# Three series of node rows in every odd step of the sorting loop instead of two in each

## The chip, the cores and the metric

The kernel runs on one NeuronCore of a Trainium2 chip. The metric is the device time of one execution in microseconds. Before the change the median of three runs was 2923.28 us (2914.42 to 2926.03). One further execution was recorded by the hardware profiler, and all rows below come from that one.

## What is computed

There are 16 graphs of 1024 nodes with 64 channels and a 0/1 adjacency matrix each. Two layers follow one another:

```python
h = relu(layernorm(x))
# layer 0, for each node: drop every skip-th neighbour, then per channel
#   sort h over the remaining neighbours (and itself), take the quantiles 0.25, 0.5, 0.75,
#   weigh them 0.25, 0.5, 0.25  -> agg
x = x + (relu((h + agg) @ W1 + b1) @ W2 + b2) * mask
# layer 1: three graph convolutions x_i = bn(relu(adj @ (x_{i-1} @ W_i) + b_i)),
h = relu(layernorm(x))
x = x + relu(concat(x1, x2, x3) @ Wl + bl)
```

The costly part is the sort of layer 0: every node sorts the values of its own neighbours, channel by channel.

## The kernel before, in words

**Pairs, blocks and series.** Graphs are handled in eight pairs (p = 0 to 7). In each graph the nodes are ranked by their number of neighbours, and places of similar rank share one sorting network (`NETS`). Places 0 to 639 and 960 to 1007 are sorted as *blocks* (`BLOCKS`, with 11, 13, 15 and 26 slots), and 1008 to 1023 as the *tail* (42 slots): TensorE picks the neighbours' values with matmuls (`gather_words`, L1215, and `gather`, L1286; VectorE makes the picking matrices at L1190 and L1255), ScalarE copies them out, and VectorE sorts with `min` and `max` (`quantiles`, L1131; products and sums at L1143 and L1152). The places 640 to 959 are sorted as *series of node rows* (`NODES`): type 0 has 17 slots, type 1 has 19, type 2 has 21. Here GpSimd fetches the neighbours' rows with indirect DMAs (`fetch_nodes`, L1413), two *asks* for one slot, and a memset of `rest_row` (L1422) as a measured pause; one slot is complete after two asks and one memset. The list of rows to ask for (`rows_listed`, L769) is the last product of `prepare` for that pair. There are 20 series: type 0 and type 1 for each pair, type 2 for each two pairs. `NODE_ORDER` (L45) says in which order they are taken.

**The loop.** For p = 0 to 6 the loop does, one after the other on VectorE: block 0, a series, block 1, block 2, a second series, in p = 4 the tails of pairs 0 to 4 as well, and block MID (the fourth block). `weave` spreads other work between the instructions of a sort: the steps of `prepare` for the next pair (by `SHARES`), the gathers of later blocks, and the asks for the next series. `asking(fetched, first, end, share)` puts that share of a series' slots evenly between two points of the sort. The first ask of a slot also waits for the sorting instruction before it (`sorted_by`), so asks don't run ahead of the sort. Both series of a step use one buffer, with the tag `gn` in `rows`: the second can't be asked for before the first is sorted. The buffer `g1` holds block 1, and afterwards block MID.

In the loop of before (L1843 to L1861) the second series is asked for during block 1 (0.4 of it) and block 2 (the rest), the MID and tail gathers are woven into block 2, and the first series of the next step is asked for at the end (0.4 beside block MID, the rest beside the next block 0). Fourteen series are sorted in the loop.

**Behind the loop.** The last pair is sorted there, and with it six series, in buffers of their own (`r0`, and two of the tag `s`). Beside them `later` (L1604) runs what is left of both layers for all eight pairs, by `LATE_SHARES` steps for each sort and the remaining steps after the last one (`ahead.rest()`). The `later` work of a pair reads `agg_d`, into which the results are written by an indirect DMA of GpSimd (`scatter`, L1312). A result of a block goes through `store` (L1319): TensorE turns it, ScalarE copies it to one of three tiles `o` (L1332), and GpSimd scatters it from there.

**Order.** Each engine carries out its instructions in the order written into its queue; a waiting instruction holds all behind it. GpSimd's queue holds the asks, their memsets, the scatters into `agg_d`, and the scatters into `live_d` and loads of `lp` (L934, L949) that `prepare` needs.

Of the kernel before, what the change touches and what calls it, by code (L numbers as in the profile page):

```python
# [10 lines left out]
F32 = mybir.dt.float32  # L11
# [13 lines left out]
P = 128  # L25
C = 64
# [3 lines left out]
MIN_DEG = 10.0  # L30
TAUS = ((0.25, 0.25), (0.5, 0.5), (0.75, 0.25))

SHARES = (20, 22, 14, 30, 9)
LATE_SHARES = (8, 8, 8, 8, 9, 9, 10, 8, 11, 8, 8)

MAGIC = 8388608.0

# [5 lines left out]
NODES = ((640, 768, 14, 17), (768, 896, 16, 19), (896, 960, 17, 21))  # L43

NODE_ORDER = (  # L45
    ((0,), 0), ((0,), 1), ((1,), 0), ((1,), 1), ((0, 1), 2), ((2,), 0), ((2,), 1), ((3,), 0), ((3,), 1), ((2, 3), 2),
    ((4,), 0), ((4,), 1), ((5,), 0), ((5,), 1), ((4, 5), 2), ((6,), 0), ((6,), 1), ((6, 7), 2), ((7,), 0), ((7,), 1),
)

LISTED = 24  # L50
# [359 lines left out]
def graph_layers_kernel(ctx: ExitStack, tc: tile.TileContext, ins, out: bass.AP):  # L410
# [889 lines left out]
    def send(pools, after=None):  # L1300

        send_nodes()
        for one in waiting:
            store(*one, pools, after)
        waiting.clear()
# [94 lines left out]
    def fetch_nodes(pairs, i, pools, tag):  # L1400

        work, ps, rows = pools
        j0, j1, _, slots = NODES[i]
        G = len(pairs) if i == 2 else 2
        pool = work if tag == "s" else keep if tag == "r0" else rows
        g = pool.tile([P, slots, G * C], F32, tag=tag, bufs=2 if tag == "s" else 1, name="g_nodes")

        def ask():
            for k in range(slots):
                for a in range(G):  # L1410
                    st = pairs[a if i == 2 else 0]
                    at = 4 if i == 2 else 2 * a + i
                    asked = nc.gpsimd.indirect_dma_start(  # L1413
                        out=g[:, k, a * C : (a + 1) * C],
                        out_offset=None,
                        in_=rows_d[st.p][:, :],
                        in_offset=bass.IndirectOffsetOnAxis(ap=st.listed[:, at, k : k + 1], axis=0),
                    )
                    if rested[0] is not None:
                        follow(asked, rested[0])  # L1420
                    if a == G - 1:
                        rested[0] = nc.gpsimd.memset(rest_row, 0.0)  # L1422
                        follow(rested[0], asked)
                    if a == 0 and sorted_by[0] is not None:
                        tc.add_manual_dep(
                            asked.ins, sorted_by[0].ins.name,
                            mybir.DependencyInfo(mybir.DependencyClass.Sync, mybir.DependencyReason.DATA),
                            reason="rows are asked for one by one",
                        )
                yield  # L1430

        z = work.tile([P, len(TAUS), G], F32, tag="z_nodes", bufs=2, name="z_nodes")
        for a in range(G):
            st = pairs[a if i == 2 else 0]
            at = 4 if i == 2 else 2 * a + i
            nc.scalar.copy(z[:, :, a : a + 1], st.nodes_z[:, :, at : at + 1])
        return pairs, i, g, z, Steps(ask())
# [12 lines left out]
    def asking(fetched, first, end, share=1.0):  # L1450

        return fetched[4], math.ceil(share * NODES[fetched[1]][3]), first, end
# [357 lines left out]
    with ExitStack() as stack:  # L1810
        keep = stack.enter_context(tc.tile_pool(name="keep", bufs=1))
        pools = (
            stack.enter_context(tc.tile_pool(name="work", bufs=1)),
            stack.enter_context(tc.tile_pool(name="ps", bufs=1, space=PSUM)),
            stack.enter_context(tc.tile_pool(name="rows", bufs=1)),
        )
        with ExitStack() as inner:
            early = (
                inner.enter_context(tc.tile_pool(name="early", bufs=1)), keep,
                inner.enter_context(tc.tile_pool(name="ps_early", bufs=1, space=PSUM)),  # L1820
            )
            ahead = Steps(prepare(0, early))
            ahead.rest()
            load_weights()
            sts = [ahead.result]
            jobs = iter(NODE_ORDER)

            def fetch_next(tag="gn"):
                pairs, i = next(jobs)
                return fetch_nodes([sts[p] for p in pairs], i, pools, tag)  # L1830

            nodes = fetch_next()
            nodes[4].rest()
            first, *_ = gather_block(sts[0], 0, pools)
            first.rest()
            for p in range(NP - 1):
                st = sts[p]
                ahead = Steps(prepare(p + 1, early))

                def steps(n):  # L1840
                    return ahead, SHARES[n], 0.0, 1.0

                weave(sort_block(st, 0, pools), gather_block(st, 1, pools), asking(nodes, 0.0, 0.9), steps(0))  # L1843
                weave(sort_nodes(nodes, pools), gather_block(st, 2, pools), steps(1))
                nodes = fetch_next()
                weave(sort_block(st, 1, pools), asking(nodes, 0.1, 1.0, 0.4), steps(2))
                send_nodes()
                both = rows_of_pairs(MID, p, p + 1, p, pools, "g1")
                weave(
                    sort_block(st, 2, pools), gather_block(st, MID, pools, into=both),  # L1850
                    gather_block(st, MID + 1, pools, (early[0], "a", 2)), asking(nodes, 0.0, 0.7), steps(3),
                )
                if p in TAILS:
                    tails = rows_of_pairs(MID + 1, *TAILS[p], TAILS[p][1], pools, "g0")
                weave(sort_nodes(nodes, pools), steps(4))
                ahead.rest()
                sts.append(ahead.result)
                nodes = fetch_next()
                if p in TAILS:
                    weave(sort_pairs(MID + 1, *TAILS[p], tails, pools))  # L1860
                    send(pools)  # L1861
                weave(
                    sort_pairs(MID, p, p + 1, both, pools), gather_block(sts[-1], 0, pools, first=0.3, end=1.0),
                    asking(nodes, 0.0, 1.0, 0.4),
                )


        with ExitStack() as inner:
            one = inner.enter_context(tc.tile_pool(name="late", bufs=1))
            late = (one, inner.enter_context(tc.tile_pool(name="ps_late", bufs=2, space=PSUM)))  # L1870
            done = Pair()
            done.sent = 4
            ahead = Steps(later(late, keep, done))
            def steps(n):
                return ahead, LATE_SHARES[n], 0.0, 1.0

            st = sts[-1]
            weave(sort_block(st, 0, pools), gather_block(st, 1, pools), asking(nodes, 0.0, 0.9), steps(0))
            weave(sort_nodes(nodes, pools), gather_block(st, 2, pools), steps(1))
            nodes = fetch_next()  # L1880
            then = [fetch_next("r0")]
            weave(sort_block(st, 1, pools), asking(nodes, 0.0, 0.9), steps(2))
            send_nodes()
            both = rows_of_pairs(MID, NP - 1, NP, NP - 1, pools, "g1")
            weave(
                sort_block(st, 2, pools), gather_block(st, MID, pools, into=both), asking(then[0], 0.0, 0.9), steps(3)
            )
            tails = rows_of_pairs(MID + 1, *TAILS[NP - 1], NP - 1, pools, "g0")
            weave(sort_nodes(nodes, pools), gather_block(st, MID + 1, pools, into=tails[:, :, -TW:]), steps(4))
            then += [fetch_next(), fetch_next("s"), fetch_next("s")]  # L1890
            weave(
                sort_pairs(MID + 1, *TAILS[NP - 1], tails, pools), asking(then[1], 0.0, 0.5), asking(then[2], 0.5, 1.0),
                steps(5),
            )
            send(pools)
            done.sent = NP - 2
            weave(sort_nodes(then[0], pools), asking(then[3], 0.0, 1.0), steps(6))
            send_nodes()
            weave(sort_pairs(MID, NP - 1, NP, both, pools), steps(7))
            send(pools)  # L1900
            weave(sort_nodes(then[1], pools), steps(8))
            send_nodes()
            done.sent = NP - 1
            weave(sort_nodes(then[2], pools), steps(9))
            send_nodes()
            weave(sort_nodes(then[3], pools), steps(10))
            send(pools)
            done.sent = NP
            ahead.rest()
# [49 lines left out]
```

## Time and profile before

| what | value |
|---|---|
| median of three runs | 2923.28 us |
| the profiled execution | 2848.07 us, its span 2846.3 us |
| mean granted TensorE clock | 0.867 |
| VectorE (DVE) busy | 2302.2 us, 81% |
| TensorE (PE) busy | 2121.2 us, 75% |
| GpSimd (POOL) busy | 1740.8 us, 61% |
| ScalarE (ACT) busy | 1659.0 us, 58% |

How to read it: times within the profiled execution are microseconds from the start of its span. The loop's first sort begins at about 238, and its steps begin at 238, 491, 761, 1029, 1280, 1605 and 1863; the part behind the loop begins at 2116. A row of groups gives line, engine, operation, names and shapes, the count, busy time and the mean of one in ns, and then the time that the engine stood idle just ahead of it with what ended the idling. A row of waits gives who waited for what: total, number of times, and the longest.

### The profile page before, as it was taken

Reading aid. Unit: us, or ns where it says so; the run is one execution under the profiler, and the core shown is the slowest. Engines: PE = TensorE matmul, PEld = TensorE weight load, DVE = VectorE, ACT = ScalarE, POOL = GpSimd, SP = SyncE. Lnnn points to the kernel's source line nnn. Section 1 sums busy time; section 2 is a strip of 40 time slices with the busy share of each in tenths; the row PEclk is TensorE's granted clock in tenths of the full one; section 3 lists DMA queues with packets and bytes.
Section 4 is the critical chain, followed back from the end, with each engine's and each line's share of the span. In section 5 each row is a group of like instructions: output and inputs, shape, how many; then the busy total and the mean of one; then the engine's idle time right before and its main releaser. Section 6 shows DMA issues by size and latency. Waiting matters only on the chain. (4 is left out here: it accounts for less than half of the span.)

```text
span 2846.3 us, 54834 instructions
## 1 busy us (share of the span) xinstructions
PE 2121.2 (75%) x21210; PEld 1375.9 (48%) x21226; DVE 2302.2 (81%) x5388; ACT 1659.0 (58%) x3325; POOL 1740.8 (61%) x1568
## 2 busy tenths in 40 slices
PE   3658977796688589869852797599777999219888
PEld 2435554454455356546531555365545566115555
DVE  3138998898989989989979898999987899419963
ACT  4795877587657857785864487767751324003322
POOL 7126665486828765673867748748691788885100
PEclk9779987898889789889966898699879899659999
DMA  4214222222313241232241222232231143212221
GB/s 127 75 50 129 65 75 69 85 63 71 94 62 89 57 132 55 75 90 75 73 81 39 62 94 67 74 104 69 66 82 22 47 62 102 43 26 70 62 61 46
DMA packets 262766, 205.43 MB, mean 72 GB/s; under 512 B 218721, under 2 KB 219105, under 8 KB 258401
## 3 DMA queue, kind: packets, MB, share of 16 engines
q1 hardware_dynamic: 182784, 134.66, 16.2%
q0 software_dynamic: 40960, 62.37, 9.1%
q10 hardware_dynamic: 38752, 4.82, 1.2%
q8 instruction: 168, 2.75, 0.4%
q14 instruction: 102, 0.83, 0.1%
HBM read 148.89 MB, written 52.81 MB: 71 GB/s over the span
## 5 line engine op out<-in xcount | busy, mean ns | idle before, releaser
L1413 POOL DMA_INDIRECT g_nodes<-rows_d,rows_listed x744 | 990.4, 1331 | 651.5 <-DVE prod L1143 276.7
L1215 PE MATMUL pg<-s,hp 128*64 128x496 fp8e4 (+5 forms) x8064 | 744.6, 336 | 159.4 <-DVE s L1190 62.0
L1215 PEld LDWEIGHTS <-hp 128*64 128x64 bf16 x8064 | 454.4, 113 | 393.6 <-ACT hp L734 83.5
L1422 POOL MEMSET rest_row<- 1x768 bf16 x372 | 295.5, 794 | 0.1
L1576 PE MATMUL pg<-adjT,xw 128*64 128x512 fp8e4 x2304 | 275.1, 388 | 3.0 <-ACT xw L1565 1.6
L1190 DVE TENSOR_SCALAR s<-r 128x3200 uint16<-128x3200 uint16 (+2 forms) x192 | 209.0, 1097 | 65.3 <-PE pg L1215 62.9
L934 POOL DMA_INDIRECT live_d<-edge,place x128 | 162.9, 1273 | 118.4 <-DVE place L926 81.4
L1219 ACT ACTIVATE g<-pg 128x400 f32<-128x400 f32 (+3 forms) x168 | 83.8, 499 | 204.5 <-PE pg L1215 171.4
L1576 PEld LDWEIGHTS <-xw 128*64 128x64 bf16 x2304 | 133.1, 112 | 129.5 <-issue 15.5
L1312 POOL DMA_INDIRECT agg_d<-o,node_of x112 | 158.1, 1412 | 51.5 <-issue 27.2
L819 ACT ACTIVATE edge<-a 128x1024 fp8e4<-128x1024 uint32 x128 | 135.4, 1058 | 89.5 <-DMA a<-in_adj 88.9
L1131 DVE TENSOR_TENSOR t_nodes<-g_nodes 128x256 f32<-128x256 f32 (+6 forms) x192 | 125.3, 663 | 69.3 <-DMA g_nodes<-rows_d,rows_listed 52.6
L875 ACT ACTIVATE stays<-cs,back 128x1024 f16<-128x1024 f32 x128 | 138.7, 1114 | 54.4 <-DVE look L856 25.2
L1131 DVE TENSOR_TENSOR t<-g 128x800 f32<-128x800 f32 (+9 forms) x184 | 168.7, 930 | 2.0
L922 ACT ACTIVATE stays<-keys,minus 128x1024 fp8e4<-128x1024 f32 x128 | 143.7, 1122 | 42.7 <-PE keys L914 38.8
L902 ACT ACTIVATE edge<-q,bias 128x1024 fp8e4<-128x1024 f32 x128 | 142.1, 1111 | 44.3 <-PE q L897 44.3
L1131 DVE TENSOR_TENSOR g<-t 128x992 f32<-128x992 f32 (+7 forms) x176 | 160.1, 935 | 2.3
L969 PE MATMUL pt<-ident_h,lp 128*128 128x128 bf16 x1024 | 108.0, 276 | 71.6 <-ACT liveT L972 30.4
L1286 PE MATMUL pg<-s,hp 128*64 128x384 bf16 (+14 forms) x1872 | 151.3, 304 | 11.1 <-DVE s L1255 11.1
L826 PE MATMUL ptE<-ident_h,one 128*128 128x128 bf16 x1024 | 84.1, 232 | 86.4 <-DVE one L823 61.4
L829 ACT ACTIVATE edgeT<-ptE 128x1024 fp8e4<-128x1024 f32 x128 | 130.4, 1027 | 21.0 <-PE ptE L826 20.1
L972 ACT ACTIVATE liveT<-pt 128x1024 fp8e4<-128x1024 f32 x128 | 124.2, 1033 | 28.6 <-PE pt L969 25.0
(261 smaller groups left out, 5055.7 us busy)
## 6 DMA issues: line engine op xcount, KB each, us to landing
a<-in_adj SPq DMA_DIRECT2D x128, 512.0 KB
lp<-live_d POOLq DMA_DIRECT2D x32, 514.0 KB
adjT_d<-edgeT SPq DMA_DIRECT2D x16, 1024.0 KB
adjT<-adjT_d SPq DMA_DIRECT2D x16, 1024.0 KB
g_nodes<-rows_d,rows_listed POOLq DMA_INDIRECT x744
room<-in_x SPq DMA_DIRECT2D x16, 256.0 KB
h_d<-room SPq DMA_DIRECT2D x16, 256.0 KB
rows_d<-room SPq DMA_DIRECT2D x64, 64.0 KB
```

Of the source, the lines that this page charges most:

```text
L875: nc.scalar.activation(stays[:, t, :], cs, AF.Abs, bias=back[:, t : t + 1], scale=2.0)
L902: nc.scalar.activation(edge[:, t, :N], q, AF.Relu, bias=bias(-2.0), accum_out=nv[:, t : t + 1], saturate=False)
L922: nc.scalar.activation(junk, keys, AF.Sign, bias=minus[:, t : t + 1], accum_out=above[:, t : t + 1], saturate=False)
L934: sent = nc.gpsimd.indirect_dma_start(out=live_d[b][:, :], out_offset=bass.IndirectOffsetOnAxis(ap=place[:, t : t + 1], axis=0), in_=edge[ ...
L1131: sorted_by[0] = nc.vector.tensor_tensor(view(bufs, o, n1, n2), view(bufs, a, n1, n2), view(bufs, b, n1, n2), ALU.max if op else ALU.min)
L1190: nc.vector.tensor_scalar(s[:, j, :, us, :], st.r[0][:, :, us, j0:j1], abs(k - 3), 0x0808, ALU.logical_shift_right if k > 3 else ALU.logic ...
L1215: summed = nc.tensor.matmul(out=pg[x * C : (x + 1) * C, those, :], lhsT=st.hp[:, part, x, u, :], rhs=picked, start=(i == 0 and part == 0), ...
L1286: summed = nc.tensor.matmul(out=pg[x * C : (x + 1) * C, ks, w0:], lhsT=st.hp[:, part, x, u, :], rhs=s[:, ks, x, u, w0:], start=(whole and ...
L1312: sent = nc.gpsimd.indirect_dma_start(out=agg_d[p][:, :], out_offset=bass.IndirectOffsetOnAxis(ap=rows, axis=0), in_=data, in_offset=None)
L1413: asked = nc.gpsimd.indirect_dma_start(out=g[:, k, a * C : (a + 1) * C], out_offset=None, in_=rows_d[st.p][:, :], in_offset=bass.IndirectO ...
L1422: rested[0] = nc.gpsimd.memset(rest_row, 0.0)
L1576: nc.tensor.matmul(out=pg[cs, :], lhsT=part[:, u, cs], rhs=adjT[x][:, u, sl], start=(u == 0 and k == 0), stop=(u == NT - 1 and k == len(xw ...
```

## The change

`NODE_ORDER` takes each two pairs' type 2 series right after the first pair of the two. In the steps p = 1, 3 and 5 a third series `more` is fetched into `g1`, between block 1 and block MID: it is asked for wholly during block 2 (and 0.2 of `nodes` with it), and sorted next; the rest of `nodes` is asked for beside that sort. The MID and tail gathers, which shared block 2's weave, stand beside the sort of `nodes` in these steps. Even steps keep their form. Seventeen series are sorted in the loop; behind it there are three: one that was already asked for, `nodes`, and a single further one, `then`, in `r0`. The tag `s` goes. `SHARES` and `LATE_SHARES` (together 65 steps instead of 99) follow.

```diff
-SHARES = (20, 22, 14, 30, 9)
-LATE_SHARES = (8, 8, 8, 8, 9, 9, 10, 8, 11, 8, 8)
+SHARES = ((20, 22, 14, 0, 30, 9), (20, 22, 14, 16, 14, 9))
+LATE_SHARES = (6, 6, 8, 8, 6, 16, 8, 7)
...
 NODE_ORDER = (
-    ((0,), 0), ((0,), 1), ((1,), 0), ((1,), 1), ((0, 1), 2), ((2,), 0), ((2,), 1), ((3,), 0), ((3,), 1), ((2, 3), 2),
-    ((4,), 0), ((4,), 1), ((5,), 0), ((5,), 1), ((4, 5), 2), ((6,), 0), ((6,), 1), ((6, 7), 2), ((7,), 0), ((7,), 1),
+    ((0,), 0), ((0,), 1), ((0, 1), 2), ((1,), 0), ((1,), 1), ((2,), 0), ((2,), 1), ((2, 3), 2), ((3,), 0), ((3,), 1),
+    ((4,), 0), ((4,), 1), ((4, 5), 2), ((5,), 0), ((5,), 1), ((6,), 0), ((6,), 1), ((6, 7), 2), ((7,), 0), ((7,), 1),
 )
...
-        pool = work if tag == "s" else keep if tag == "r0" else rows
-        g = pool.tile([P, slots, G * C], F32, tag=tag, bufs=2 if tag == "s" else 1, name="g_nodes")
+        pool = keep if tag == "r0" else rows
+        g = pool.tile([P, slots, G * C], F32, tag=tag, bufs=1, name="g_nodes")
...
                 weave(sort_nodes(nodes, pools), gather_block(st, 2, pools), steps(1))
+                more = fetch_next("g1") if p % 2 else None
                 nodes = fetch_next()
                 weave(sort_block(st, 1, pools), asking(nodes, 0.1, 1.0, 0.4), steps(2))
                 send_nodes()
+                if more is not None:
+                    weave(
+                        sort_block(st, 2, pools), asking(more, 0.0, 0.9), asking(nodes, 0.1, 0.9, 0.2), steps(3)
+                    )
+                    weave(sort_nodes(more, pools), asking(nodes, 0.0, 0.8), steps(4))
+                    send_nodes()
                 both = rows_of_pairs(MID, p, p + 1, p, pools, "g1")
-                weave(
-                    sort_block(st, 2, pools), gather_block(st, MID, pools, into=both),
-                    gather_block(st, MID + 1, pools, (early[0], "a", 2)), asking(nodes, 0.0, 0.7), steps(3),
+                small = (
+                    gather_block(st, MID, pools, into=both), gather_block(st, MID + 1, pools, (early[0], "a", 2)),
                 )
+                if more is None:
+                    weave(sort_block(st, 2, pools), *small, asking(nodes, 0.0, 0.7), steps(4))
+                    small = ()
...
-                weave(sort_nodes(nodes, pools), steps(4))
+                weave(sort_nodes(nodes, pools), *small, steps(5))
...
             nodes = fetch_next()
-            then = [fetch_next("r0")]
+            then = fetch_next("r0")
             weave(sort_block(st, 1, pools), asking(nodes, 0.0, 0.9), steps(2))
...
+            weave(sort_block(st, 2, pools), gather_block(st, MID, pools, into=both), asking(then, 0.0, 1.0, 0.7), steps(3))
+            tails = rows_of_pairs(MID + 1, *TAILS[NP - 1], NP - 1, pools, "g0")
             weave(
-                sort_block(st, 2, pools), gather_block(st, MID, pools, into=both), asking(then[0], 0.0, 0.9), steps(3)
+                sort_nodes(nodes, pools), gather_block(st, MID + 1, pools, into=tails[:, :, -TW:]),
+                asking(then, 0.0, 1.0), steps(4),
             )
-            tails = rows_of_pairs(MID + 1, *TAILS[NP - 1], NP - 1, pools, "g0")
-            weave(sort_nodes(nodes, pools), gather_block(st, MID + 1, pools, into=tails[:, :, -TW:]), steps(4))
-            then += [fetch_next(), fetch_next("s"), fetch_next("s")]
-            weave(
-                sort_pairs(MID + 1, *TAILS[NP - 1], tails, pools), asking(then[1], 0.0, 0.5), asking(then[2], 0.5, 1.0),
-                steps(5),
-            )
+            weave(sort_pairs(MID + 1, *TAILS[NP - 1], tails, pools), steps(5))
             send(pools)
-            done.sent = NP - 2
-            weave(sort_nodes(then[0], pools), asking(then[3], 0.0, 1.0), steps(6))
+            done.sent = NP - 1
+            weave(sort_nodes(then, pools), steps(6))
             send_nodes()
             weave(sort_pairs(MID, NP - 1, NP, both, pools), steps(7))
-            send(pools)
-            weave(sort_nodes(then[1], pools), steps(8))
-            send_nodes()
-            done.sent = NP - 1
-            weave(sort_nodes(then[2], pools), steps(9))
-            send_nodes()
-            weave(sort_nodes(then[3], pools), steps(10))
             send(pools)
```

More of the change, by code (lines that the diff above doesn't have):

```diff
@@ L1840, in steps @@
                 def steps(n):
-                    return ahead, SHARES[n], 0.0, 1.0
+                    return ahead, SHARES[p % 2][n], 0.0, 1.0
                 weave(sort_block(st, 0, pools), gather_block(st, 1, pools), asking(nodes, 0.0, 0.9), steps(0))
                 weave(sort_nodes(nodes, pools), gather_block(st, 2, pools), steps(1))
+                more = fetch_next("g1") if p % 2 else None
                 nodes = fetch_next()
```

## The prediction

> **What bounds the kernel now.** I read the engines' totals first, then a table of stretches, then the waits, and last the timeline of the one large hole.
>
> ```profile
> PE 2121.2 (75%) x21210; PEld 1375.9 (48%) x21226; DVE 2302.2 (81%) x5388; ACT 1659.0 (58%) x3325; POOL 1740.8 (61%) x1568
> ```
>
> No engine fills the span, so the stretches have to say who limits where (columns: length, busy time of PE, PEld, DVE, ACT, POOL with counts, PE clock, DMA share, GB/s). The first two rows are loop steps p = 1 and p = 3; the others lie behind the loop.
>
> ```profile
> 491.00:761.00 270.00, 205.22 (x2200) 132.34 (x2200) 234.40 (x538) 186.18 (x371) 195.18 (x166) 0.87 0.27 77
> 1029.00:1280.00 251.00, 204.03 (x2236) 134.35 (x2234) 236.29 (x539) 186.51 (x371) 159.08 (x144) 0.90 0.28 81
> ...
> 2454.00:2545.00 91.00, 2.74 (x25) 1.20 (x21) 0.18 (x1) 1.05 (x3) 77.42 (x90) 0.54 0.11 20
> 2545.00:2611.00 66.00, 57.12 (x421) 36.33 (x423) 59.77 (x164) 23.90 (x62) 47.48 (x40) 0.88 0.38 86
> 2611.00:2735.00 124.00, 103.62 (x797) 64.70 (x794) 121.30 (x236) 34.84 (x66) 11.33 (x6) 0.93 0.21 57
> 2735.00:2846.00 111.00, 100.49 (x823) 61.91 (x822) 41.11 (x61) 28.48 (x47) 1.92 (x2) 0.96 0.17 45
> ```
>
> In the loop VectorE is busy 1700.6 of 1878 us (the seven steps summed), 91%. Behind it TensorE is the busiest, except from 2454 to 2545, where only GpSimd works. The timelines of ScalarE and VectorE show what ends that hole:
>
> ```profile
> 2543.95 0.26 ACT L1332 COPY o<-pt_agg 16x128 f32<-16x128 f32 x1 [94.73 <-DMA agg_d<-o,node_of]
> ```
>
> ```profile
> 2544.82 0.55 DVE L1581 TENSOR_SCALAR xT<-xT,bn_s,c_L_gnn_be 128x512 f32<-128x512 f32 x1 [91.10 <-ACT xT L1580]
> ```
>
> After the tails' sort, `send` copies four turned aggregates into three tiles `o`. The fourth copy waits until a tile's scatter has left, and that scatter stands in GpSimd's queue behind the asks of `then[1]` and `then[2]`. ScalarE holds up everything else: 91 us lost.
>
> GpSimd's queue also matters in the loop. These are its groups from the start of block 1 to the start of the second series, p = 3, and then the same queue in the hole:
>
> ```profile
> L1413 POOL DMA_INDIRECT g_nodes<-rows_d,rows_listed x33 | 38.3, 1160 | 7.9 <-issue 6.4 <-DVE g L1131 0.6 <-DVE stays L876 0.3
> L1422 POOL MEMSET rest_row<- 1x768 bf16 x17 | 14.4, 848 | 0.0
> ```
>
> ```profile
> L1413 POOL DMA_INDIRECT g_nodes<-rows_d,rows_listed x47 | 44.5, 948 | 10.3 <-issue 10.3
> L1422 POOL MEMSET rest_row<- 1x768 bf16 x28 | 20.4, 727 | 0.0
> ```
>
> One slot is two asks and a memset: 2 x (1.160 + 7.9/33) + 0.848 = 3.65 us in the loop, 2 x (0.948 + 10.3/47) + 0.727 = 3.06 us when VectorE stands still. In p = 1 the same sum is 4.06 (asks of 1.378). Nearly all idle time is "issue", not a wait for the sort: from 1097 to 1185 GpSimd works without a break of note (17 slots at 3.65 = 62, `live_d` scatters and loads 14, results 7, of 88 us), while VectorE is busy 85.4. Both are full there.
>
> **The change, part by part, in the time of the profiled execution (2848.07, span 2846.3).**
>
> *The hole goes: -91.* Behind the loop only `then` is asked for early, its last slots beside the sort of `nodes`. From block 1 on GpSimd has 17 + 14 slots, and 5 more in the next stretch, 36 x 3.65 = 131 us, for stretches that took some 150 (block 1, block 2, a series). Nothing is queued when the tails are sent, 76 us later. Bounds: -91, or -86 if the four tails' eight scatters (1.1 us median) hold a copy.
>
> *Three series fewer behind the loop: about 0.* Their VectorE time isn't on the path. Before, 68 `later` steps are issued through block MID (2611) and 53 run from there to the end, in 236 us with three series beside them. After, 65 are issued by then and 56 remain, exactly the last four pairs. The undisturbed period of a pair is read from the chain: pair 6's first matmul of L1560 at 2734.6, pair 7's at 2791.4, the end at 2846.3: 56.8, and 54.9 for the last. Four pairs: 3 x 56.8 + 54.9 = 225, plus up to 15 for steps issued and not yet run. That is 225 to 240 against 236. The three series were hidden beside TensorE, and what stands ahead of 2611 keeps its three sorts.
>
> *Three series more in the loop.* By VectorE alone: five stretches of series in the loop hold 146.6 us of L1131, 29.3 each; with products and sums (51 us over 20 series) 32. Types 2, 0 and 1 move in, so 3 x 32 = 96, beside which nothing is idle.
>
> By GpSimd it is more. In an odd step, before `more` can be sorted, GpSimd has 8 slots of `nodes`, 17 of `more` and 4 of `nodes`: 29 x 3.65 = 106, two results 4, eight `live_d` 10 to 12: 120 us from block 1's start. VectorE gets there sooner than before: 88 minus the gathers' L1255 (14.4 us, moved behind) = 74. Stall: 46. `more` then takes 32 + 3, and the remaining 7 slots with the other scatters 37, so `nodes` starts at 157 and, with L1255 beside it (32 + 14), ends at 203. Before, the same two stretches took 88 + 28 = 116. That is +87, with every stall empty. If asks speed up to 3.06 while VectorE waits, 29 slots take 89, the stall is 31, and the end is at 183: +67. If it is VectorE's work alone: +32. I take +67, the value nearest to rows: 3 x 67 = 201. First-series sorts in odd steps are now type 2, longer in VectorE: +20 over the three; even steps lose 13 (type 0 and 1 only) and p = 4 loses its one wait for a late type 2 (14.4): -27.
>
> *Fresh lists.* Every first series of a step now belongs to a pair whose `rows_listed` (L769) has only just been made, at 456, 728, 995, 1245, 1518, 1829 and 2083. Before, that held for p = 1 alone, where 34 asks ran from 457 to 535 (79 us with the scatters between) and the sort waited 11.7 us. Type 2 takes four slots more, +16. Against the old start of that sort: p = 1 +15, p = 2 +5, p = 3 (995 + 95 = 1090, was 1057) +28 to 33, p = 4 (1324, was 1308) +16, p = 5 none (the tails' sort gives time), p = 6 (1908, was 1891) +17; behind the loop (2178, was 2156) +22. Loop 81; I take 70, as asks quicken in a stall, and 13 of 22 behind. Bounds: 0, if `prepare` is then earlier, and 103.
>
> A rule speaks against all this. The Trainium skill, "SBUF — State Buffer", "A bandwidth-pool intuition that's wrong (but worth ruling out)", says that a DMA whose descriptors GpSimd writes goes from some 620 ns alone to some 3100 beside certain VectorE instructions, since one locks the other out. Five times longer would make a slot 2 x 3.1 + 0.8 = 7 us and the 29 slots 203. The row says 1160 or 1378 against 948, 1.2 to 1.45 times. I keep the row.
>
> *Moved at no cost:* MID and tail gathers (some 19 us of PE) lie beside a sort; without that cover block MID would wait up to 19. `prepare`'s shares only move.
>
> Sum: -91 + 0 + 13 behind the loop; 201 + 20 - 27 + 70 = 264 within: +186, a profiled execution of 3034. The median of the runs is 2923.28, 2.6% above the profiled one; I add the difference to it: 3109, put at 3105.
>
> **The rivals.**
>
> *Faster (0.15):* the loop swallows the series. Its VectorE idles 177 us; if asks keep ahead and the new work fills half its own length, the loop costs 96 - 48 = 48, and -91 remains: -43, 2880. It decides as soon as the loop grows by under 91. Against it: GpSimd has no pause between block 1 and the second series.
>
> *No change (0.08):* VectorE's sum alone, 96 - 91 = +5: 2928.
>
> *Slower, empty stalls (0.17, with the case that the hole stays elsewhere):* 3 x 87 + 20 - 27 + 81 - 91 + 22 = +266: 3189.
>
> *Mine (0.60):* between +70 and +240.
>
> The range 2905 to 3205 leaves out the better part of the gain's tail and the worst of the last. Half a per cent, 15 us, is about what a measurement of this kernel can tell from no change. Slower 0.77, same 0.08, faster 0.15.
>
> **What would show it.** The step 2454 to 2545 has no counterpart (ACT `o` waits under 10 us at a time). From the last sort to the end about 230 us. VectorE's waits for DMA `g_nodes`, 36.4 us in the loop now, rise above 150; odd steps take 320 to 350, even ones 255 to 275. I am wrong if odd steps stay under 300: then GpSimd wasn't full, or VectorE found other work.

## The result and the profile after

The kernel after takes 3162.52 us (median of 4 runs, 3153.01 to 3177.12) where the kernel before takes 2924.66 (4 runs, 2914.42 to 2928.91): a ratio of 1.0823, 95% interval 1.077 to 1.0877. That is +238 us; the forecast was +186 in the profiled execution, and the time lies in the range. Its profiled execution took 3153.01, with a span of 3151.2 at a mean granted clock of 0.833.

The recorded execution of before (2848.07) ran at a higher granted clock than most later ones, 0.90 against 0.86 in step p = 0, which is almost the same program in both, so steps of after are compared below with `b_late`, an experiment whose loop is that of before, run at 0.87 in that step.

The engines' busy times have hardly changed; the span has grown around them:

```profile
PE 2166.5 (69%) x21207; PEld 1387.6 (44%) x21226; DVE 2289.1 (73%) x5388; ACT 1663.8 (53%) x3325; POOL 1720.9 (55%) x1568
```

VectorE does the same 5388 instructions in about the same time and stands idle for 862 us instead of 544. The view of waits says for what (who waits for what: total, times, longest):

```profile
DVE t_nodes L1131 <- DMA g_nodes<-rows_d,rows_listed: 280.7, 11, 48.9
...
POOL g_nodes L1413 <- DVE rows_listed L769: 158.1, 6, 44.7
...
ACT g_pairs L1291 <- DVE prod L1143: 106.7, 2, 57.7
...
ACT o L1332 <- DMA agg_d<-o,node_of: 79.3, 5, 42.7
```

The first row was 52.6 before, the second 22.0 (once). VectorE waits for rows, and GpSimd waits six times for a list that has only just been made. The last row was 116.7, of which 94.7 were the hole behind the loop; what is left has two new places, shown below.

The table of stretches, in after for the steps p = 1 to 6 and for all that lies behind the loop (columns as in the prediction):

```profile
516.60:866.50 349.90, 215.49 (x2243) 135.97 (x2242) 259.42 (x595) 181.11 (x363) 229.69 (x196) 0.79 0.20 57
866.50:1154.50 288.00, 211.89 (x2176) 133.26 (x2180) 236.45 (x542) 195.09 (x394) 176.12 (x154) 0.82 0.27 77
1154.50:1513.80 359.30, 214.35 (x2248) 135.14 (x2246) 261.02 (x595) 181.19 (x363) 238.06 (x204) 0.78 0.20 56
1513.80:1876.10 362.30, 219.81 (x2237) 142.71 (x2241) 283.73 (x730) 196.18 (x410) 244.86 (x192) 0.78 0.25 62
1876.10:2207.60 331.50, 206.00 (x2214) 135.85 (x2214) 260.68 (x605) 189.67 (x389) 207.64 (x167) 0.81 0.23 65
2207.60:2494.30 286.70, 211.57 (x2156) 133.42 (x2156) 228.53 (x534) 187.31 (x380) 180.03 (x157) 0.84 0.28 77
2494.30:3151.20 656.90, 549.45 (x4557) 351.82 (x4553) 445.67 (x901) 179.86 (x367) 187.87 (x178) 0.91 0.23 53
```

The same steps p = 1 and p = 3 in `b_late`, with the loop of before:

```profile
520.20:801.20 281.00, 212.71 (x2224) 134.88 (x2222) 237.15 (x538) 186.47 (x372) 195.83 (x177) 0.83 0.26 75
...
1070.40:1336.10 265.70, 208.80 (x2216) 138.84 (x2214) 234.88 (x538) 186.04 (x370) 158.15 (x144) 0.88 0.27 77
```

An odd step has 22 to 26 us more VectorE work (259.4 against 237.2, 261.0 against 234.9) and is 63 to 93 longer. Step by step, measured from block 0 to block 0:

| us | p=0 | 1 | 2 | 3 | 4 | 5 | 6 | loop | behind |
|---|---|---|---|---|---|---|---|---|---|
| loop of before (`b_late`) | 268 | 281 | 269 | 266 | 315 | 268 | 264 | 1931 | |
| after | 273 | 350 | 288 | 359 | 362 | 332 | 287 | 2250 | 657 |
| difference | +5 | +69 | +19 | +93 | +47 | +63 | +23 | +319 | |

Behind the loop the program of before took 730 in the recorded execution and 729 in `b_o4`, which changes it little: after is 73 shorter there. 319 - 73 = 246, against the 238 of the medians.

How far single traces can be trusted: the four experiments `b_late`, `b_late2`, `b_late3` and `b_o4` have the loop of before (`b_o4` with one more tile). In them it took 1931 to 1957, step p = 4 took 314 to 335, and every other step agreed within 12 us. A difference of one step by less than that says little.

What an odd step looks like inside: VectorE's timeline in p = 3 of after, at the start of the third series,

```profile
1341.99 0.43 DVE L1131 TENSOR_TENSOR t_nodes<-g_nodes 128x256 f32<-128x256 f32 x1 [6.53 <-DMA g_nodes<-rows_d,rows_listed]
...
1394.31 2.36 DVE L1131 TENSOR_TENSOR t_nodes<-g_nodes 128x1024 f32<-128x1024 f32 x2 [48.94 <-DMA g_nodes<-rows_d,rows_listed]
```

and GpSimd's groups from the first ask of that stretch (1257) to the end of that wait (1394.3):

```profile
L1413 POOL DMA_INDIRECT g_nodes<-rows_d,rows_listed x65 | 73.5, 1131 | 64.5 <-DVE prod L1143 49.5 <-issue 13.6 <-DVE coef L1152 0.3
L1422 POOL MEMSET rest_row<- 1x768 bf16 x34 | 24.9, 733 | 0.0
L934 POOL DMA_INDIRECT live_d<-edge,place x8 | 11.8, 1474 | 2.4 <-issue 2.4
```

Of the 64.5 us of idle time 49.5 lie ahead of the first ask at 1258.5; from there on GpSimd has no break for 136 us, while VectorE has 74.5 us of work up to 1345 and then 0.4 us in the 49 that follow. ScalarE pays too: its copy into `g_pairs` (the row of 57.7 among the waits) needs the buffer `g1`, which the third series holds until it is sorted.

The step p = 4 has a hole that the loop of before did not have. GpSimd at the end of p = 4:

```profile
1761.08 1.02 POOL L1413 DMA_INDIRECT g_nodes<-rows_d,rows_listed  x1 [24.88 <-DVE rows_listed L769]
...
1770.37 11.38 POOL L1413 DMA_INDIRECT g_nodes<-rows_d,rows_listed  x1 [0.16 <-issue]
...
1810.59 16.68 POOL L1413 DMA_INDIRECT g_nodes<-rows_d,rows_listed  x1 [0.16 <-issue]
...
1828.16 0.95 POOL L1413 DMA_INDIRECT g_nodes<-rows_d,rows_listed  x1 [0.16 <-issue]
...
1847.79 0.87 POOL L1312 DMA_INDIRECT agg_d<-o,node_of  x1 [0.30 <-issue]
```

and ScalarE and VectorE behind it:

```profile
1851.02 0.25 ACT L1332 COPY o<-pt_agg 16x128 f32<-16x128 f32 x1 [42.74 <-DMA agg_d<-o,node_of]
```

```profile
1868.37 0.99 DVE L1190 TENSOR_SCALAR s<-r 128x3200 uint16<-128x3200 uint16 x1 [41.48 <-remote]
```

It is the hole of before once more, at the other place where tails are sent. The list is ready at 1761; 22 asks follow without a wait, 21 of them with a memset behind each: these are the second asks of all 21 slots, since only the first ask of a slot waits for the sort. The tails' scatters stand behind them, the fourth copy to `o` waits for a scatter, and VectorE stands for 41.5 us.

A smaller hole of the same kind stands behind the loop, where results of the last pair's blocks are sent. ScalarE there:

```profile
2741.38 0.27 ACT L1332 COPY o<-pt_agg 128x128 f32<-128x128 f32 x1 [21.55 <-DMA agg_d<-o,node_of]
```

From 2719.8 to 2737.8 GpSimd makes 13 asks for `then` ahead of the scatter that this copy waits for, and VectorE works 1.3 of the 21.6 us.

### The profile page after: what moved, and what is told of

It reads as the page before. It is cut to its first block, busy times and chain, and to the rows that moved or that the text cites. A ratio compares the mean times of both kernels' runs of the same rounds, so it can differ in the third digit from the quotient of the medians.

```text
span 3151.2 us, 54846 instructions
## 1 busy us (share of the span) xinstructions
PE 2166.5 (69%) x21207; PEld 1387.6 (44%) x21226; DVE 2289.1 (73%) x5388; ACT 1663.8 (53%) x3325; POOL 1720.9 (55%) x1568
## 5 line engine op out<-in xcount | busy, mean ns | idle before, releaser
L1413 POOL DMA_INDIRECT g_nodes<-rows_d,rows_listed x744 | 997.3, 1341 | 730.8 <-DVE prod L1143 257.3
L1215 PE MATMUL pg<-s,hp 128*64 128x496 fp8e4 (+5 forms) x8064 | 769.4, 344 | 215.3 <-DVE s L1190 96.1
L1215 PEld LDWEIGHTS <-hp 128*64 128x64 bf16 x8064 | 467.4, 116 | 461.1 <-issue 106.9
L1131 DVE TENSOR_TENSOR t_nodes<-g_nodes 128x256 f32<-128x256 f32 (+5 forms) x192 | 124.5, 659 | 286.1 <-DMA g_nodes<-rows_d,rows_listed 280.7
L1576 PE MATMUL pg<-adjT,xw 128*64 128x512 fp8e4 x2304 | 281.2, 389 | 15.7 <-ACT xw L1565 5.9
L1422 POOL MEMSET rest_row<- 1x768 bf16 x372 | 288.0, 774 | 0.1
L1312 POOL DMA_INDIRECT agg_d<-o,node_of x112 | 127.9, 1142 | 239.1 <-ACT o L1332 207.2
L1576 PEld LDWEIGHTS <-xw 128*64 128x64 bf16 x2304 | 140.3, 112 | 134.4 <-issue 23.5
L1021 PE MATMUL pr<-liveT,upto 128*128 128x512 fp8e4 (+1 forms) x256 | 89.1, 371 | 143.3 <-ACT g_pairs L1291 105.8
L1286 PE MATMUL pg<-s,hp 128*64 128x384 bf16 (+14 forms) x1872 | 167.2, 311 | 20.4 <-issue 12.5
L1131 DVE TENSOR_TENSOR t<-g 128x800 f32<-128x800 f32 (+9 forms) x184 | 167.9, 926 | 1.5
L1131 DVE TENSOR_TENSOR g<-t 128x992 f32<-128x992 f32 (+7 forms) x176 | 159.9, 933 | 1.8
L969 PEld LDWEIGHTS <-lp 128*128 128x128 fp8e4 x1024 | 87.0, 122 | 156.4 <-issue 88.3
```

What stands on the lines that cost most here:

```text
L969: nc.tensor.matmul(out=pt[:, u, :], lhsT=lp[:, u * P : (u + 1) * P], rhs=ident_h, start=True, stop=True)
L1131: sorted_by[0] = nc.vector.tensor_tensor(view(bufs, o, n1, n2), view(bufs, a, n1, n2), view(bufs, b, n1, n2), ALU.max if op else ALU.min)
L1215: summed = nc.tensor.matmul(out=pg[x * C : (x + 1) * C, those, :], lhsT=st.hp[:, part, x, u, :], rhs=picked, start=(i == 0 and part == 0), ...
L1286: summed = nc.tensor.matmul(out=pg[x * C : (x + 1) * C, ks, w0:], lhsT=st.hp[:, part, x, u, :], rhs=s[:, ks, x, u, w0:], start=(whole and ...
L1413: asked = nc.gpsimd.indirect_dma_start(out=g[:, k, a * C : (a + 1) * C], out_offset=None, in_=rows_d[st.p][:, :], in_offset=bass.IndirectO ...
L1576: nc.tensor.matmul(out=pg[cs, :], lhsT=part[:, u, cs], rhs=adjT[x][:, u, sl], start=(u == 0 and k == 0), stop=(u == NT - 1 and k == len(xw ...
```

## The experiments

The theory: the third series costs its asks, GpSimd being full between block 1 and that series, and the fresh lists cost the rest. The rivals: the buffer `g1` that delays block MID's gathers; VectorE's own work; and, for the gain, that the hole behind the loop goes by another arrangement of asks alone.

**Asks left out (`a_noasks`).**

```diff
         def ask():
+            if tag == "g1":
+                nc.vector.memset(g, 1.0)
+                return
```

> The changed kernel with the asks of the third series (34 in each of three steps) left out; one memset of VectorE fills its tile, so those aggregates are not the reference's. VectorE's sort stays. If the asks cost the time, the waits of about 55 us before the third series go and the steps lose 55 to 70 us each: about 2960 to 3000. If VectorE's own work of the third series (32 us each) is the cost, almost nothing changes: above 3130.

Measured: 3007.76, ratio 1.0316 (1.0256 to 1.0377), 155 less than after. The loop took 2094, 157 less; odd steps 308, 309 and 283, so 27, 44 and 15 above the loop of before, where they were 69, 93 and 63. VectorE's waits for rows halve:

```profile
DVE t_nodes L1131 <- DMA g_nodes<-rows_d,rows_listed: 146.2, 9, 32.8
```

Some 47 us of each odd step (42 to 50) come from the asks of one series; the other 16 of the 157 were lost in p = 2 and p = 6.

**The sort left out, the asks kept (`a_nosort`).**

```diff
-                    weave(sort_nodes(more, pools), asking(nodes, 0.0, 0.8), steps(4))
+                    def first_slot(fetched):
+                        fetched[4].rest()
...
+                        nc.vector.tensor_copy(agg, fetched[2][:, 0, :])
...
+                    weave(first_slot(more), asking(nodes, 0.0, 0.8), steps(4))
```

> The changed kernel with all asks of the third series, but without its sort: its first slot is copied to the output, so those aggregates are not the reference's. VectorE has 32 us less in three steps and doesn't wait for the last asks. If the asks set the pace, the second series still waits behind them, and only part is won: 90 to 150 us, about 3040. If VectorE's work is what counts, the steps fall by the 32 and the 55 us of waiting each, 260 in all: about 2900.

Measured: 3130.42, ratio 1.0725 (1.0674 to 1.0776), only 32 less than after and less than either theory expected. Odd steps took 359, 364 and 342, no shorter than with the sort (350, 359, 332). The loop as a whole lost 24, nearly all of it in p = 2 (21) and p = 6 (15), and why there stays open. Without asks an odd step falls by 47, without the sort by nothing: GpSimd sets its pace, and VectorE's own work does not.

**The third series in another buffer (`a_own`).**

```diff
-                more = fetch_next("g1") if p % 2 else None
+                more = fetch_next("s") if p % 2 else None
```

> The changed kernel with the third series in a buffer of the gathers (tag s) instead of g1, so that block MID's first copy on ScalarE need not wait until that series is sorted. If GpSimd's asks set the odd steps' length, the wait of VectorE before the third series (about 55 us a step) stays, only prepare gets on beside it and the next list comes some 20 us earlier: 30 to 60 us less, about 3115. If the copy waiting for g1 is the cause, 55 us of each odd step go: about 3000.

Measured: 3183.62, ratio 1.0919 (1.0864 to 1.0974), some 21 more than after, where both theories of the expectation had it faster. The wait for rows stays, and the copy of block MID waits for TensorE instead of for `g1`:

```profile
DVE t_nodes L1131 <- DMA g_nodes<-rows_d,rows_listed: 289.3, 11, 49.6
...
ACT g_pairs L1291 <- PE pg L1286: 117.4, 7, 54.5
```

So `g1` is not what VectorE waits for: in p = 3 it waits 48.7 us for rows where the copy has no such buffer to wait for (48.9 in after). But block MID's gathers did not get ahead. TensorE's matmul waited 57.3 us for a picking matrix, which VectorE makes only behind its own wait; also, the tag `s` is no buffer of the series' own but the two tiles that the picking matrices take in turn (L1186, L1252). In both kernels TensorE and ScalarE stand for some 55 us in p = 3, and work of `prepare` stands behind them. What that costs by itself no run shows, nor why this one is slower.

**An older list for the first series of a step (`a_stale`).**

```diff
-                nodes = fetch_next()
+                nodes = fetch_next(lists=sts[p])
...
-                        in_offset=bass.IndirectOffsetOnAxis(ap=st.listed[:, at, k : k + 1], axis=0),
+                        in_offset=bass.IndirectOffsetOnAxis(ap=(lists or st).listed[:, at, k : k + 1], axis=0),
```

> The changed kernel, but the series that is fetched at the end of a step takes its row numbers from the list of the pair before, which has long been made; so many asks and sorts as before, but the rows of those series are not the reference's. If the fresh list delays each step's first sort, VectorE's waits for the first series (10 to 24 us in six steps) mostly go and the time falls by 50 to 85 us: about 3090. If GpSimd's queue is simply full, asks that start earlier only wait elsewhere: above 3140.

Measured: 3065.93, ratio 1.0502 (1.0445 to 1.0559), 97 less than after. By steps: p = 1 -19, p = 2 -8, p = 3 -25, p = 4 -48, p = 5 +6, p = 6 +5, behind the loop -22. More than half of what the loop gains lies in p = 4, whose hole is gone: the longest wait of a copy to `o` at the tails is 9.0 us.

**The hole in p = 4 by a fourth tile (`a_o4`), and by asks that wait (`a_tied`).** The first gives the copies a fourth tile and pays for it with a smaller `rest_row` (its memset still takes 0.77 us):

```diff
-        o = work.tile([P, P], F32, tag="o", bufs=3, name="o")
+        o = work.tile([P, P], F32, tag="o", bufs=4, name="o")
```

> The changed kernel with four tiles o instead of three; the pause writes 768 bytes instead of 768 bf16 to make room. At the end of step 4 five results are stored behind the asks for a type 2 series, and the fourth copy on ScalarE stood 42.7 us in the trace of the changed kernel. If that copy holds up the step, about 40 us go: 3120. If VectorE would have waited for the asks anyway, nothing: 3162.

Measured: 3132.29, ratio 1.0732 (1.066 to 1.0804), 30 less. But p = 4 became 32 shorter and p = 5 became 25 longer, and the loop as a whole lost 5. The part behind the loop lost 20, from 657 to 636: with four tiles no copy waits for a scatter there, so the hole of 21.55 has gone.

The second lets both asks of a slot wait for the sort in the one series fetched ahead of those tails:

```diff
-                    if a == 0 and sorted_by[0] is not None:
+                    if (a == 0 or tie) and sorted_by[0] is not None:
...
-                nodes = fetch_next()
+                nodes = fetch_next(tie=p in TAILS)
```

> The kernel after, in which both asks of a slot (not only the first) wait for the sort, in the one series that is fetched ahead of the tails of pairs 0 to 4 (end of p = 4). In the kernel after, 21 second asks of that series are let go at 1761 us beside the tails' sort, ten of them take 1.6 to 16.7 us instead of 0.95, and the tails' scatters stand behind them until 1848: VectorE idle 41.5 us. Theory 1 (the hole is a loss of its own, made by asks that ran ahead): p = 4 takes 316 to 325 us instead of 362, the idle time before L1190 at its end is under 5 us, the first series of p = 5 waits at most 15 us longer, and the whole is 25 to 42 us shorter (ratio to the kernel before 1.068 to 1.074). Theory 2 (GpSimd is full there, the asks have to be made at some time): p = 4 is shorter by 35 or so, p = 5 longer by 25 or more, as with four tiles for the copies, and the whole moves by less than 12.

Measured: 3105.96, ratio 1.0914 (1.0881 to 1.0947) to a kernel before that took 2847.53 beside it (granted clock 0.90 in p = 0, as in the recorded execution of before); so its total can't be set against that of after. Its steps can, where they differ by much: p = 4 took 318, p = 5 took 380 (after: 362 and 332). The wait stands at the first series of p = 5 now:

```profile
1877.76 1.49 DVE L1131 TENSOR_TENSOR t_nodes<-g_nodes 128x1280 f32<-128x1280 f32 x1 [40.15 <-DMA g_nodes<-rows_d,rows_listed]
```

p = 4 and p = 5 together: 694 in after, 686 with four tiles, 698 here, and 652 with the older list. By the steps, theory 2 of that expectation holds: those asks have to be made at some time, and GpSimd has no slack there. The hole is the form that the fresh list takes in p = 4, not a loss of its own.

In this kernel the steps p = 0 and 2 ran at a granted clock of 0.90 and 0.86 (0.86 and 0.82 in after) and were 22 and 14 us shorter; p = 1 and 3 ran at 0.79 and 0.77 (0.79 and 0.78) and were 10 and 2 longer. Against the kernel before, this one costs 258 us where after costs 238; what share of that is the clock's, no run shows.

**No pauses between the asks (`a_norest`).**

```diff
-                    if a == G - 1:
+                    if False:
                         rested[0] = nc.gpsimd.memset(rest_row, 0.0)
```

> The changed kernel without the memsets of rest_row between the slots: a slot is two asks, about 0.8 us shorter. If GpSimd's queue is what the odd steps wait for, each of them gains 29 x 0.8 = 22 us before the third series, and the waits for a first series shrink by some 15 us in six places: about 3030 to 3060. If the queue isn't the limit, nothing: 3162. If the pauses protect other transfers, the time rises above 3162.

Measured: 3226.61, ratio 1.1034 (1.095 to 1.1118), 64 more than after. The first expectation, 3030 to 3060, failed in its sign; a rise was its last case, there put down to other transfers. GpSimd lost 276 us of work and the waits of VectorE for rows fell to 40.3, but TensorE stood idle. From the waits of `a_norest`:

```profile
PEld L1215 <- issue: 327.6, 396, 8.7
...
PE pg L1215 <- issue: 196.1, 255, 2.6
```

The first row is 106.9 in after and 59.8 in before, the second 15.7 in after; the two can count the same time. TensorE's timeline beside a run of asks:

```profile
389.65 0.31 PE L1215 MATMUL pg<-s,hp 128*64 128x248 fp8e4 x2 [1.03 <-issue]
391.10 0.37 PE L1215 MATMUL pg<-s,hp 128*64 128x248 fp8e4 x3 [1.14 <-issue]
392.52 0.57 PE L1215 MATMUL pg<-s,hp 128*64 128x248 fp8e4 x3 [1.04 <-issue]
```

A gap of about 1 us for each two or three matmuls, with nothing to wait for that the profile shows. So the pauses, 288 us of GpSimd's time, can't simply be dropped to end the stall: without them TensorE loses more than GpSimd gains.

**The gain alone: the loop of before, the hole taken away (`b_late`, `b_late2`, `b_late3`, `b_o4`).** Six series stay behind the loop; what changes is when `then` is asked for.

```diff
-            weave(
-                sort_pairs(MID + 1, *TAILS[NP - 1], tails, pools), asking(then[1], 0.0, 0.5), asking(then[2], 0.5, 1.0),
-                steps(5),
-            )
+            weave(sort_pairs(MID + 1, *TAILS[NP - 1], tails, pools), asking(then[1], 0.0, 0.9), steps(5))
```

That, with `then[2]` and `then[3]` each beside later sorts, is `b_late`.

> The kernel before, with the asks behind the loop put off: then[1] beside the tails' sort, then[2] half beside the sort of then[0] and half beside block MID, then[3] beside the sort of then[1]. The loop is untouched. If GpSimd's queue made the 91 us hole, it goes and the time falls by 80 to 91: about 2840 us. If the hole only moves (the series now come late for their own sorts), the time stays within 20 us of 2924. The loop's steps also show how long they are in a second profile of the same program: 253 to 270 us for an ordinary one.

Measured: 2895.66, ratio 0.9934 (0.9906 to 0.9962), so about 19 won instead of 80 to 91. The wait of the copy to `o` falls from 94.7 to 52.6 and does not go.

`b_late2` moves the asks for `then[2]` out of the series' sort into block MID and later.

> As the variant with later asks (2896), but then[2] is asked for only from block MID on, so that no asks stand before the tails' scatters; then[3] follows beside the sorts of then[1] and then[2]. The 51 us hole that was left in that variant should go: 2896 - 45 = about 2850. If the asks then come too late for the last two series, their sorts wait and the time stays near 2895.

Measured: 2885.96, ratio 0.9868 (0.9818 to 0.9918); 46.8 of the wait remain. Asks for `then[2]` that are second in their slot don't wait for the sort: 17 of them ran ahead of the tails' scatters, although they were written beside a later sort.

`b_late3` ties both asks of a slot to the sort in these series and asks for 0.7 of `then[1]` only ahead of the tails' results:

```diff
-                    if a == 0 and sorted_by[0] is not None:
+                    if (a == 0 or tag == "s") and sorted_by[0] is not None:
...
+            weave(sort_pairs(MID + 1, *TAILS[NP - 1], tails, pools), asking(then[1], 0.0, 0.8, 0.7), steps(5))
...
+            weave(sort_nodes(then[0], pools), asking(then[1], 0.5, 1.0), steps(6))
```

> As the variant that asks for then[2] from block MID on (2886), but now both asks of a slot wait for the sort in the tag s series (the second one was free, and 17 of them had run ahead of the tails' scatters), and 0.3 of then[1] is asked for behind the send. If asks ahead of the scatters make the hole, the 45 us that were left of it shrink below 15: about 2850. If the hole stays, the asks weren't its cause, and the time stays near 2886.

Measured: 2869.05, ratio 0.9828 (0.9773 to 0.9883) to the kernel before, the shortest of the three, though its interval overlaps that of `b_late2`. So 53 us of the 91 can be had with the loop as it was. The longest wait of a copy to `o` behind the loop:

```profile
2447.22 0.27 ACT L1332 COPY o<-pt_agg 128x128 f32<-128x128 f32 x1 [9.79 <-DMA agg_d<-o,node_of]
```

The part behind the loop took 666 with six series in it; in after it takes 657 with three. Moving three series out of it brought only 9 us on balance, since after has two new losses there, the fresh list (22 by `a_stale`) and the hole of 21.55 (20 by `a_o4`).

`b_o4` leaves the asks as in before and gives the copies four tiles, as above.

> The kernel before with four tiles o instead of three (and the shorter pause tile). If the copy on ScalarE alone makes the 91 us hole behind the loop, it goes: about 2830. If the layers' next step needs the scatters themselves, which stay behind the asks, VectorE stands at the sum of L1518 instead and little is won: above 2890.

Measured: 2912.11, ratio 0.9957 (0.9934 to 0.9981). The hole stays, at another engine:

```profile
2625.42 1.23 DVE L1518 TENSOR_TENSOR agg<-agg,h_late 128x1024 f32<-128x1024 f32 x1 [93.51 <-issue]
```

The late layers need what the scatters write, so the copy's tile was only the first to show it.

**One series fewer in the loop (`b_13`).** On top of `b_late3`, p = 6 sorts a single series and a seventh follows behind the loop.

```diff
+                one_only = p == NP - 2
...
-                weave(sort_nodes(nodes, pools), steps(4))
+                if not one_only:
+                    weave(sort_nodes(nodes, pools), steps(4))
```

> As the last, but step 6 of the loop sorts one series instead of two, and seven are left behind the loop. If a series costs its time in the loop (50 us or more with its asks) and is hidden beside TensorE behind it, 15 to 40 us are won on the last variant. If the part behind the loop is full as well, with 121 of 124 us of VectorE busy between 2611 and 2735, the series costs 32 us there and the balance is within 15 us.

Measured: 2933.4, ratio 1.0055 (1.002 to 1.009), 64 more than `b_late3`, which neither theory expected. Step p = 6 took 263, no less than in `b_late` (264), and the part behind the loop 754, 88 more, with four waits for rows of 4.3 to 27.2 us, 69 in all. So a seventh series is far from free behind the loop. Why p = 6 did not get shorter without one stays open.

## Why the prediction was right in its direction and short in its size

**Behind the loop: right in its sum, by luck in its terms.** The forecast was -91 + 0 + 13 = -78; measured -73. The hole at the tails has gone: their four copies to `o` wait 2.5 us at most, and from the last sort's end (2931) to the end (3151) are 220 us (225 to 240 forecast). But "Nothing is queued when the tails are sent" looked at the tails alone. Asks for `then` stand ahead of other scatters there, which makes the hole of 21.55, and the first series waits 27.5 where 13 were reckoned. And "Three series fewer behind the loop: about 0" was too small a gain: without the two new losses after would take some 615 there, an estimate from 657, 22 (`a_stale`) and 20 (`a_o4`), which no run removed together. That is some 50 less than the 666 of `b_late3`. Two losses hid it.

**Odd steps: the mechanism held, the stall was too small.** The sum had 3 x 67 = 201, made of 32 for VectorE and 35 for the stall, 105 for three. By `a_noasks` the asks of the third series take 140 in the three odd steps and 157 in the loop. The step that failed is "If asks speed up to 3.06 while VectorE waits, 29 slots take 89, the stall is 31, and the end is at 183": it gives the quick pace to all 29 slots. In p = 3 asks do quicken to 0.95 us, but only from 1345 on, when VectorE has stopped; 33 of the 65 asks had begun by then, at 1.31 each. From 1258.5 to 1394.3 are 136 us, with 65 asks and 34 memsets instead of 58 and 29 (some of the next slots' had come ahead); VectorE's wait is 6.5 + 48.9 = 55, against 46 for the slow pace and 31 for the fast. The value "every stall empty", 87 for a step, was the nearer one.

VectorE's part was put too high. With the "+20" for longer first series the forecast gives odd steps 116 us more work; they have 74. The loop as a whole has 67 more (1766 against 1699 in `b_late`), where 103 were forecast. The 29.3 for one series came from stretches in which L1131 also worked for blocks; by its own instructions a series takes VectorE some 25, 28 or 33 us, by type. (The slot of p = 1, given as 4.06, comes out at 3.96 from its rows; nothing rests on it.)

**Fresh lists: right in sum, wrong in place.** Forecast 70 in the loop and 13 behind it; `a_stale` gives 90 and 22 by steps, 97 by the medians. But p = 4 was put at +16, with 14.4 given back, and it is 48. The prediction had read the order of GpSimd's queue (scatters behind asks) only at the tails behind the loop; the same stands at the tails of pairs 0 to 4, where the change newly puts asks that come late, and `a_stale` has no hole there. It also gave even steps as 255 to 275, without the tails' sort that makes p = 4 longer in any case (315 in the loop of before).

The forecast had set a rule aside. The Trainium skill, "SBUF — State Buffer", "A bandwidth-pool intuition that's wrong (but worth ruling out)", has a DMA fed by GpSimd go from 620 to 3100 ns beside certain VectorE instructions; the forecast kept the 1.2 to 1.45 times of the rows. Over all 744 asks that was right: 1341 ns in after, 1331 in before, 1.4 times the 948 of the hole. In the stretch from 1761 to 1827, beside the tails' sort, it wasn't:

```profile
L1413 POOL DMA_INDIRECT g_nodes<-rows_d,rows_listed x11 | 57.3, 5212 | 26.5 <-DVE rows_listed L769 24.9 <-issue 1.6
```

That is 5.2 us for one, 5.5 times the 0.95 that the next eleven took when VectorE stood still, with single ones of 11.4 and 16.7. By an estimate from these numbers those eleven would have taken 47 us less at 0.95, and the queue would have been through at about 1800, ahead of the tails' end at 1827. No run took the VectorE work away beside these asks, so the lock itself is argued and not shown.

**The sum.** Put side by side, 157 for the asks of the third series, 90 for the lists and 67 for VectorE make 314, and the loop grew by 319. The forecast had 105, 70 and 103, with 14 given back in p = 4: 264. So the asks were short by 52 and the lists by 20, VectorE was over by 36, and the 14 did not come back. That the terms add up is argued and not shown: no run removed two of them at once, the sort left out with the asks in place gave 24 in the loop and not 67, and a loop of one and the same program moves by up to 26 from trace to trace.

**The rivals.** *Faster*: out, since GpSimd had no room between the first series' sort and the third's; 53 us of the gain that it counted on were to be had without the change in the loop (`b_late3`). *No change*: out by `a_nosort`, since VectorE's work is not what the odd steps wait for. *Slower, empty stalls*, 3189: its stalls are nearer to the measured ones, and the result is nearer to it (27 off) than to the forecast (58). One more was not tried: just ahead of the 136 us GpSimd stood idle for 49.5 (257 in the whole execution, six times), since the asks that came next in its queue needed the buffer `gn`, which the first series still held. A third series in a buffer that is free by then might be asked for in that time; no run does it.

**What was to show it.** VectorE's waits for rows rose from 36.4 in the loop to 253 (280.7 less the 27.5 behind it), above the 150 said; odd steps took 332 to 359 where 320 to 350 was said. Two signs failed. Copies to `o` were to wait under 10 us at a time; one waits 42.7 and one 21.55. And even steps took 288, 362 and 287 against 255 to 275. For p = 4 that is the hole. In p = 2 and 6 (269 and 264 in `b_late`) the first series waits 19.3 and 14.0, but the older list of `a_stale` takes only 8 off p = 2 and nothing off p = 6, whose wait is 14.1 there too; so most of that growth stays open.

## What to carry to other kernels

A queue that runs without a pause in the stretch that others wait for is full there, whatever its average share: moving work to where another engine has idle time gains nothing if that idle time is spent waiting for this queue. When an in-order queue is given other work, look at every place where a short instruction stands behind it, not only at the one that the change is about; and if one such wait is removed, count the next step too before calling it a gain. Often the better part of a change is the removal of a wait, which can be had alone.

## What was not expected of the hardware

Asks on GpSimd without pauses slow TensorE. With one memset for each slot TensorE's time lost to "issue" at the weight loads of L1215 is 107 us (after), without them 328 us; at the matmuls there it is 16 and 196. The whole is 64 us longer although GpSimd has 276 us less to do. What lies behind these gaps no run shows. And the time of one ask beside VectorE has a very wide spread, 1.0 to 16.7 us in one stretch, so that its mean over a kernel (1.34) says little of a stretch on the path.
